# A later load of the second batch's expert results, and a copy that takes the attention numerators out of their bank

## The chip, the cores and the metric

The kernel runs on one core of one Trainium2 chip. The metric is the device time of one execution in microseconds. The engines are named as the profile names them: PE is TensorE, PEld its weight loads, DVE is VectorE, ACT is ScalarE, POOL is GpSimd and SP is SyncE, which issues most of the transfers.

## The reference, cut to what matters

`x` is (4, 512, 256) in float32. Two residual branches are added to it, one after the other. The first is a layer of experts followed by a linear attention, and the change lies where the one hands over to the other. The second (an attention with a field term, and two layers of local attention with a gated feed-forward) takes the larger part of the time and is not touched.

```python
def _L0_cond_ref(x, ...):                       # experts
    ...
    topk_w, topk_i = jax.lax.top_k(gate_w, TOP_K)               # 2 of 8 experts for each row
    cw = jnp.sum(jax.nn.one_hot(topk_i, E, dtype=x.dtype) * topk_w[..., None], axis=-2)
    h1 = jax.nn.relu(jnp.einsum('bsh,ehm->bsem', x, W1) + b1)
    h2 = jax.nn.relu(jnp.einsum('bsem,emn->bsen', h1, W2) + b2)
    out_e = jnp.einsum('bsen,enh->bseh', h2, W3) + b3
    return jnp.einsum('bseh,bse->bsh', out_e, cw)

def _L0_attn_ref(x, w_qkv, w_out, b_out, proj):  # linear attention, 8 heads of 32, blocks of 32 rows
    ...
    qp = jax.nn.elu(jnp.einsum('bhcsd,hdf->bhcsf', q, proj)) + 1.0
    kp = jax.nn.elu(jnp.einsum('bhcsd,hdf->bhcsf', k, proj)) + 1.0
    kv = jnp.einsum('bhcsf,bhcsd->bhcfd', kp, v)
    num = jnp.einsum('bhcsf,bhcfd->bhcsd', qp, kv)
    ksum = kp.sum(axis=3)
    z = 1.0 / (jnp.einsum('bhcsf,bhcf->bhcs', qp, ksum) + 1e-08)
    out = num * z[..., None]
    ...
    return out @ w_out.T + b_out

x = x + _L0_attn_ref(_L0_cond_ref(x, ...), ...)
x = x + _L0_ffn_ref(_L0_cond2_ref(x, ...), ...)
return x
```

## The kernel before

**The work and its stages.** There are four batches of 512 rows of 256 numbers, and each batch is four tiles of 128 rows (`NT`). From 0 to 317 us the experts run: rows are gathered for each expert, three layers are multiplied through, and GpSimd's indirect transfers (L1470) put each result row where it belongs in the DRAM tensor `ys`. While the last of these results travel, TensorE is kept busy by filler multiplications (`busy`, tile `pbusy`), which read `xres[0]`, batch 0's residual. From 317 to 349 us lies what this text calls the opening: the results are loaded back and batch 0's part of the linear attention begins. The linear attention fills 349 to 482 us, the attention with the field term 482 to 715, and the local attention with the feed-forward 715 to 1376.

**Loading and summing the results.** `results(b)` (L1525) makes the tiles `g0` and `g1` of 128 x 4 x 256, one for each of a row's two experts, and loads them from `ys` (L1532). Each tag has two buffers, so batches 0 and 1 can be loaded at once, while batch 2 waits until batch 0's tiles are free and batch 3 until batch 1's are. Batch 0 is loaded in four transfers of two tiles (256 KB each), those of `g1` on ScalarE's queue and those of `g0` on SyncE's; the others are loaded in two transfers of 512 KB, both on SyncE's. `weighted(b)` (L1536) then does, for each of the four tiles, one ScalarE multiplication (L1539, in place in `g0`, by the first expert's weight) and one VectorE operation that adds `g1` times the second weight and writes `y[b]`, the tile that the profile calls `ymoe` (L1540). At L1543 both batch 0's and batch 1's loads are issued, and after them batch 0's sums (L1544).

**The linear attention.** `front(b, d)` (L1556) is run for each batch: it makes the batch's sums (batch 0's are already made), issues the loads of batch b + 2, has GpSimd add the output bias to `xres[b]` (L1561, tile `xres`), transposes `y[b]` on TensorE (`pt` to `yT`) and multiplies by the weights (`pqk` to `qk`, `pv` to `v`). `evac` copies a PSUM bank to SBUF, in turn on ScalarE (L123) and on VectorE (L125). `features` multiplies each head's query or key by its projection (`pf`, two banks), and makes the feature of it with two ScalarE activations (`ex`, L1599 and L1600) and one VectorE operation that reads `pf` and `ex` (`f`, L1602). `scores` multiplies features by features (`psc`), and VectorE masks the product to the blocks (`sc`, L1612). `values(d, g)` takes a group of four heads: TensorE fills one bank with the numerators (`pn`) and one with the denominators (`pz`), ScalarE adds 1e-8 to the denominators (`z`, L1631), VectorE takes the reciprocal in place (L1636), and VectorE multiplies `pn` by it into `aT` (L1637). The last group of the last batch does these last two in halves. `tail` multiplies `aT` by the output weights (`pao`), and VectorE adds that to `xres` (L1647).

**What sets the order.** The order of TensorE's instructions is the program's own, pinned by `PE.in_order()` and `tc.keep_in_program_order`. The work of the next batch (`front`) and of the one before (`tail`) is handed out in steps by `beside(b)` between a batch's `features`, `scores` and `values`. Beside the last batch stand the first pieces of the next stage (`pck`, `pcq`, `pct`, `pcv`, and the field term's `fterm` operations on GpSimd, L390 and L391). The order on the other engines is chosen by a scheduler when the program is built, and it also chooses which bank a tile gets. All of `pt`, `pqk`, `pv`, `psc`, `pn`, `pz` and `pao` share four PSUM banks (kind `mm`); `pf` has its own two buffers of two banks. A matmul into a bank must wait for the last reader of what was in it.

## Time and profile before

| | |
|---|---|
| Time, median of three runs | 1381.41 us (1377.8 to 1935.3) |
| The profiled execution's own time | 1378.49 us |
| Its span in the trace | 1376.6 us |
| Mean granted TensorE clock | 0.994 of full speed |
| Instructions | 19525 |
| Bytes moved by the DMA engines | 94.74 MB |
| Busy in 317 to 349 us (32 us): PE, DVE, ACT | 28.95, 18.33, 20.03 us |
| Busy in 349 to 482 us (133 us): PE, DVE, ACT | 126.02, 96.95, 68.42 us |
| Busy in 482 to 715 us (233 us): PE, DVE, ACT | 230.03, 74.79, 137.61 us |

The profiled execution's time is the span of the trace and 1.9 us around it. The last three rows are read as what an engine worked within a stretch: the difference to the stretch's length is what it waited or stood without work. A name such as "pqk L78 <- DVE aT L1637" in a list of waits says that the instruction at line 78 which writes `pqk` was released by the VectorE instruction at line 1637 which writes `aT`. Line 78 is the helper that records every matmul, line 82 the one that records every transpose, so these are told apart by their tiles.

### The profile page before, as it was taken

The page shows a single profiled execution, that of the slowest core. Times are in us where ns is not written, and L with a number is a line of the kernel's source. Part 1 is how long each engine was busy: PE and PEld are TensorE (multiplying, and loading weights), DVE is VectorE, ACT ScalarE, POOL GpSimd, SP SyncE. Part 2 cuts the span into 40 slices and gives each one's busy share as a digit, 9 for nine tenths or more (in the row PEclk, how much of TensorE's full clock was granted, in tenths as well). Part 3 has the DMA queues.
Part 4 walks back from the last instruction along what each step waited for, and adds up shares of the span by engine and source line. Part 5 has one row for each costly group of instructions (what it writes and reads, how often), then busy time and mean ns, then how long its engine had stood idle before and what let it go on. Part 6 is the DMA issues. An engine that isn't in the chain of part 4 may idle for free.

```text
span 1376.6 us, 19525 instructions
## 1 busy us (share of the span) xinstructions
PE 1336.3 (97%) x7628; PEld 830.3 (60%) x7628; DVE 653.6 (47%) x1295; ACT 595.8 (43%) x1125; POOL 232.3 (17%) x223
## 2 busy tenths in 40 slices
PE   5999999999999999999999999999999999999998
PEld 4788888884566633433345556656555565556654
DVE  6222121225777743332237697653361777854421
ACT  4111111115555365565656755662222666574111
POOL 1324322211000021010103132000030322310110
PEclk8999999999999999999999999999999999999999
DMA  4577767543000000000220001211001010011000
GB/s 140 208 243 270 238 227 249 192 148 130 1 1 1 1 1 1 1 1 0 89 73 1 18 25 32 86 32 24 24 0 42 24 33 25 17 41 44 20 24 25
DMA packets 43086, 94.74 MB, mean 69 GB/s; under 512 B 9569, under 2 KB 25065, under 8 KB 40169
## 3 DMA queue, kind: packets, MB, share of 16 engines
q1 hardware_dynamic: 37560, 81.81, 18.3%
q0 software_dynamic: 3792, 10.24, 2.3%
q10 hardware_dynamic: 1632, 1.34, 0.3%
q8 instruction: 63, 1.03, 0.3%
q14 instruction: 39, 0.31, 0.1%
HBM read 84.08 MB, written 7.21 MB: 66 GB/s over the span
## 4 chain that ended last, share of the span: by engine, by line
PE 89%; DVE 5%; ACT 2%; DMA 1%; issue 1%; SPq 0%; POOLq 0%; POOL 0%; DVEq 0%
PE ph L78 14%; PE pdq L78 12%; PE pfy L78 6%; PE pug L78 5%; PE sc L78 5%; PE pua L78 5%; PE pv L78 5%; PE po L78 5%; PE pn L78 4%; PE pdy L78 4%; PE pds L78 4%; PE pz L78 2%; PE pqt L82 2%; PE pqk L78 1%; PE pck L78 1%
## 5 line engine op out<-in xcount | busy, mean ns | idle before, releaser
L78 PE MATMUL pdq<-wqkv,yT 128*128 128x512 f32 x384 | 177.1, 603 | 0.2 <-ACT yT L602 0.2
L420 ACT ACTIVATE cex<-sc 128x512 f32<-128x512 f32 x256 | 132.2, 603 | 85.5 <-PE sc L78 85.5
L78 PE MATMUL ph<-h,w 128*128 128x256 f32 (+1 forms) x704 | 132.8, 346 | 1.0 <-issue 1.0
L628 POOL TENSOR_TENSOR qr<-t,t 128x512 f32<-128x512 f32 x64 | 85.9, 1342 | 266.2 <-DVE t L625 225.2
L672 DVE TENSOR_TENSOR p<-p,lmask 128x384 f32<-128x384 f32 (+1 forms) x128 | 92.2, 735 | 69.4 <-ACT p L670 68.2
L78 PEld LDWEIGHTS ph<-h,w 128*128 128x128 f32 x704 | 116.1, 191 | 13.1 <-issue 1.3
L1402 ACT ACTIVATE h<-ph,w 128x256 f32<-128x256 f32 (+1 forms) x88 | 35.4, 438 | 190.7 <-PE ph L78 128.6
L78 PEld LDWEIGHTS pdq<-wqkv,yT 128*128 128x128 f32 x384 | 69.7, 190 | 78.4 <-issue 72.6
L670 ACT ACTIVATE p<-pds,ss 128x256 f32<-128x256 f32 (+1 forms) x256 | 96.1, 457 | 39.1 <-PE pds L78 30.7
L1404 DVE TENSOR_SCALAR h<-ph,w 128x256 f32<-128x256 f32 (+1 forms) x88 | 36.1, 438 | 160.3 <-PE ph L78 102.6
L78 PE MATMUL sc<-qm,kT 32*128 32x512 f32 x512 | 80.6, 639 | 0.0
L78 PE MATMUL pug<-hT,w 128*128 128x512 f32 x160 | 76.8, 602 | 0.0
L618 ACT ACTIVATE sq<-pdq 128x512 f32<-128x512 f32 x64 | 38.3, 598 | 85.4 <-PE pdq L78 47.7
L78 PE MATMUL pua<-hT,w 128*128 128x512 f32 x160 | 75.2, 592 | 0.0
L78 PE MATMUL ph<-xbT,w 128*128 128x256 f32 (+1 forms) x352 | 68.8, 347 | 0.6 <-ACT xbT L123 0.5
L78 PE MATMUL pv<-cex,v 128*32 128x512 f32 x512 | 68.6, 604 | 0.0
L390 POOL TENSOR_SCALAR fterm<-vw,faT 128x256 f32<-128x256 f32 x16 | 14.6, 925 | 316.2 <-DVE cr L380 316.2
L78 PE MATMUL po<-w,h 128*128 128x256 f32 x296 | 67.6, 379 | 0.0
L78 PE MATMUL pds<-qT,kT 64*128 64x256 f32 (+1 forms) x512 | 65.3, 375 | 0.0
L78 PEld LDWEIGHTS pds<-qT,kT 64*128 64x128 f32 x512 | 43.9, 186 | 32.9 <-issue 25.8
L78 PEld LDWEIGHTS ph<-xbT,w 128*128 128x128 f32 x352 | 58.5, 191 | 7.6 <-issue 0.8
L78 PE MATMUL pdy<-wo,oT 128*128 128x256 f32 x256 | 61.5, 386 | 0.0
(301 smaller groups left out, 2130.3 us busy)
## 6 DMA issues: line engine op xcount, KB each, us to landing
w<-in_moe_w_dram SPq DMA_DIRECT2D x22, 1024.0 KB
w<-in_moe_w_dram SPq DMA_DIRECT2D x22, 640.0 KB
w<-in_moe_w_dram SPq DMA_DIRECT2D x22, 516.0 KB
zb<-rows SPq DMA_DIRECT2D x32, 256.0 KB
g<-ys SPq DMA_DIRECT2D x6, 512.0 KB
wqkv<-in_f_wqkv_dram SPq DMA_DIRECT2D x2, 1536.0 KB
w<-in_f_w_dram SPq DMA_DIRECT2D x2, 1408.0 KB
out_dram<-yc SPq DMA_DIRECT2D x16, 128.0 KB
```

The lines of the kernel that those rows point to most:

```text
L78: cls._queue(nc.tensor.matmul(*args, **kw))
L82: cls._queue(nc.tensor.transpose(*args, **kw))
L390: nc.gpsimd.tensor_scalar_mul(fterm[:, t, :], vw, W["faT"][:, t, b : b + 1])
L420: nc.scalar.activation(ex[:, i, :], pss[2 * j + i], AF.Exp, scale=CHD**-0.5)
L618: nc.scalar.activation(sq, p3, AF.Square)
L628: nc.gpsimd.tensor_tensor(qr_t[:, s], t1, t2, ALU.add)
L670: nc.scalar.activation(p[:, at], pss[r][:, at], AF.Exp, scale=d.ss[:, 2 * u + jj, 1, 2 * c + r : 2 * c + r + 1])
L672: nc.vector.tensor_tensor(p[:, :n], p[:, :n], lmask[:, :n], ALU.mult)
L1402: nc.scalar.activation(dst, src, AF.Relu, bias=bias)
L1404: nc.vector.tensor_scalar(dst, src, bias, 0.0, ALU.add, ALU.max)
```

## The change

Two edits. First, batch 1's loads are issued behind batch 0's first two sums, where they were issued before any of the sums. Two one-element VectorE memsets into batch 1's tiles, pinned in program order, stand before the loads, so that the loads wait for them; and the load of `g1` goes to ScalarE's queue, where it was on SyncE's. `weighted` takes the tiles to be summed as an argument. Second, in `values`, ScalarE copies the numerators `pn` to `aT` in SBUF; VectorE multiplies `aT` in place by the reciprocals, where it multiplied from `pn`'s bank.

```diff
             def results(b):
                 gs = [gp.tile([128, NT, H], F32, tag=f"g{k}", name=f"g{k}", bufs=2) for k in range(2)]
+                if b == 1:
+
+                    for k in range(2):
+                        tc.keep_in_program_order(nc.vector.memset(gs[k][0:1, 0, 0:1], 0.0))
                 n = 2 if b == 0 else NT
...
-                        queue = nc.scalar if b == 0 and k == 1 else nc.sync
+                        queue = nc.scalar if b < 2 and k == 1 else nc.sync
...
-            def weighted(b, gs):
-                for t in range(NT):
+            def weighted(b, gs, at=range(NT)):
+                for t in at:
...
-            both = {b: results(b) for b in range(2)}
-            weighted(0, both[0])
+            both = {0: results(0)}
+            weighted(0, both[0], range(2))
+            both[1] = results(1)
+            weighted(0, both[0], range(2, NT))
...
                 nc.scalar.activation(z, pz, AF.Identity, bias=eps8)
 
+                nc.scalar.copy(d.aT[:, g, :], pn)
+
                 n = S // 2 if d is ds[-1] and g == 1 else S
                 for at in range(0, S, n):
                     half = slice(at, at + n)
                     nc.vector.reciprocal(z[:, half], z[:, half])
-                    nc.vector.tensor_tensor(d.aT[:, g, half], pn[:, half], z[:, half], ALU.mult)
+                    nc.vector.tensor_tensor(d.aT[:, g, half], d.aT[:, g, half], z[:, half], ALU.mult)
```

As the program is built, the order of TensorE's instructions is the same with the change as without it. On ScalarE the copy to `aT` stands ahead of `z` in all eight groups, although the code has it behind. On VectorE the memsets stand behind the last copy of the experts' stage (`faT`) and ahead of batch 0's third sum; batch 1's four sums stand ahead of the copy of `qk`; and in batch 3's first group both of the features `f` stand ahead of the addition to `xres`, where one of them stood behind it. With the change line numbers after L1525 move up: `aT` is copied at L1639 and multiplied at L1645, `z` is at L1637, its reciprocal at L1644, `f` at L1608, `sc` at L1618, `xres` at L1655, the loads at L1536 and the sums at L1544.

## The prediction

> **What bounds the kernel now.** The page first: TensorE is busy 97% of the span and carries 89% of the chain that ended last, so only a change in TensorE's own gaps or clock moves the end.

> ```profile
> PE 1336.3 (97%) x7628; PEld 830.3 (60%) x7628; DVE 653.6 (47%) x1295; ACT 595.8 (43%) x1125; POOL 232.3 (17%) x223
> PE 89%; DVE 5%; ACT 2%; DMA 1%; issue 1%; SPq 0%; POOLq 0%; POOL 0%; DVEq 0%
> ```

> Second, what TensorE waited for between 315 and 490 us, where both edits lie (columns: total us, times, longest). These six waits, 6.7 us in all, are what the change can aim at: under 0.5% of the span. Whatever it does, the reader should expect single microseconds.

> ```profile
> PE pt L82 <- DVE ymoe L1540: 2.3, 1, 2.3
> PE pqk L78 <- DVE aT L1637: 1.9, 2, 1.0
> PE pck L78 <- DVE aT L1637: 1.3, 1, 1.3
> PE pqk L78 <- DVE yT L125: 1.2, 2, 0.6
> ```

> Third, the opening, us by us (after the comma: busy of PE, PEld, DVE, ACT, POOL; clock; DMA share; GB/s), and the instructions in it.

> ```profile
> 321.00:322.00 1.00, 1.00 (x4) 0.28 (x2) 0.82 (x3) 0.59 (x3) 0.00 (x0) 1.00 1.08 374
> 323.00:324.00 1.00, 0.00 (x0) 0.00 (x0) 1.00 (x1) 0.01 (x1) 1.00 (x1) 1.00 1.09 385
> 325.00:326.00 1.00, 0.93 (x5) 0.88 (x5) 0.07 (x1) 0.61 (x2) 0.00 (x0) 0.50 0.00 0
> ```
> ```profile
> 322.06 2.34 POOL L1561 TENSOR_TENSOR xres<-xres,crows 128x1024 f32<-128x1024 f32 x1 [5.20 <-DMA g<-ys]
> 322.49 2.58 DVE L1540 SCALAR_TENSOR_TENSOR ymoe<-g,m,g 128x256 f32<-128x256 f32 x2 [0.35 <-ACT g L1539]
> 324.73 1.73 PE L82 MATMUL pt<-ident,ymoe 128*128 128x128 f32 x6 [2.29 <-DVE ymoe L1540]
> ```

> See that TensorE waits 2.29 us for batch 0's third and fourth sums, which take 2.58 together: one took 2.18 (the longest of the sixteen, whose median is 0.48) and ended 0.3 after GpSimd's addition, which it overlaps all along. The wait is for that addition, not for a load. After it the granted clock is 0.50 until 328.2, so eight pqk matmuls take 4.7 us where the next eight take 3.7.

> Fourth, the second numerator group of batch 0 (its twin is at 406-414), and the end of the stage.

> ```profile
> 371.05 0.69 ACT L1631 ACTIVATE z<-pz,eps 128x512 f32<-128x512 f32 x1 [3.06 <-PE pz L78]
> 371.77 3.35 DVE L1636 RECIPROCAL z<-z 128x512 f32<-128x512 f32 x1 [1.94 <-ACT z L1631]
> 375.22 0.69 DVE L1637 TENSOR_TENSOR aT<-pn,z 128x512 f32<-128x512 f32 x1
> 375.83 1.22 DVE L1602 SCALAR_TENSOR_TENSOR f<-pf,ex 128x1024 f32<-128x1024 f32 x1
> 376.96 0.68 DVE L125 COPY yT<-pt 128x512 f32<-128x512 f32 x1
> ...
> 375.97 1.12 PE L78 MATMUL pqk<-yT,awqkv 128*128 128x512 f32 x2 [0.96 <-DVE aT L1637]
> 377.70 1.12 PE L78 MATMUL pqk<-yT,awqkv 128*128 128x512 f32 x2 [0.60 <-DVE yT L125]
> ...
> 466.16 0.68 DVE L1647 TENSOR_TENSOR xres<-pao,xres 128x512 f32<-128x512 f32 x1
> 467.31 1.89 PE L78 MATMUL pcv<-cwqkv,xT 128*128 128x256 f32 x8
> ```

> See that the reciprocal, the multiplication, f and yT are one unbroken VectorE run from 371.77 on. TensorE waits for its second link (aT, which frees pn's bank) and then for its fourth (yT): taking the first wait away leaves the other. The last two rows show pcv starting 0.47 us after the xres that frees its bank.

> **The loads.** Removed: batch 1's transfers beside batch 0's. The microseconds from 318 moved 47, 303, 382 and 374 GB/s, 1.08 MB by 321.93, when batch 0's last half (1.05 MB in all) had landed: batch 1 had taken some 0.03 MB, 0.1 us. And the sum that follows waits for GpSimd, whose addition starts at 322.06 when TensorE's fillers end (321.96). Two memsets join VectorE after faT (321.98): a two-column operation takes 0.16, so 0.3 us, before a sum that is held to 324.4 anyway. If a memset is held too, that sum starts 0.3 later: 0 to +0.3; reductions and PSUM copies ran at their usual 0.69 beside GpSimd's work at 542-547, so I take 0.

> Added: later landings. SP's issue goes behind a memset, ScalarE's behind its fourth multiplication and a memset: about 322.4 and 322.9, where ScalarE is idle until 325.68, so its 0.47 is hidden. From batch 0's first issue (317.40) to its last landing (321.93) were 4.5 us; batch 1's is then at 327.0, where it was 324.6. Behind it on ScalarE: three multiplications (0.46 apart), then the qk copy, done by 329.4; TensorE's pf needs it at 330.95. Then a fourth, at 329.5, and batch 2's four (landing 329.2 as now, its SP issue still waiting for 325.1) until 331.6; ex, released by pf, starts at 332.13. Batch 3 is issued once batch 1's buffers are free: 330.5 for 328.8, so its last landing moves from 334.06 to at most 335.8; its first sum stands before f2 on VectorE, which ScalarE releases at 336.77. All hidden, with 1.5, 0.5 and 0.5 us of cover. If a cover goes, each us late is a us of TensorE. In return the VectorE qk copy moves from 331.44, behind batch 2's sums, to 331.05, but f2 is still ScalarE's: -0.4 to +1.5, taken -0.1. No indirect transfer on GpSimd's queue stands behind the loads.

> **The numerators.** Added: eight ScalarE copies of 128x512, 0.57 to 0.59 each by the qk and yT rows, ahead of z. The next ScalarE operation starts 0.48 after such a copy starts. pn ends 0.2 to 0.3 before pz, so z, and the VectorE run behind it, comes later by 0.26, 0.18, 0.19, 0.19 (pn ends at 370.76, 406.23, 441.79, 458.73; z started at 371.05, 406.60, 442.15, 459.09). The multiplication with both inputs in SBUF costs what it did: p<-p,lmask of 128x512 takes 0.69 too.

> By group, from each one's rows: the first groups of batches 0, 1 and 2 leave no TensorE gap and the shift ends in slack: 0. Second groups of batches 0 and 1: pqk's first half no longer waits 0.96, but its second half needs yT, now 0.26 (0.18) later: +0.26, +0.18. That of batch 2: pck's 1.27 goes, but pf's second half waits for the f that ended at 450.22: +0.19. First group of batch 3: the built order has xres behind the second f. It ended at 466.84 with 0.47 to spare before pcv; f's step is 1.13, plus 0.19: +0.85. Second group of batch 3: the second sc had waited for z (482.69); its bank now waits for the copy, 482.4: -0.3. So the waits named aT, 3.2 us, become waits for yT, f and xres.

> [...]

> Sum: -0.1 + 0.26 + 0.18 + 0.19 + 0.85 - 0.3 = +1.1. The profiled execution took 1378.5 (span 1376.6 and 1.9 around it), 2.9 under the median: 1379.6, given as 1380.

> **The rivals.**
> 1. *Clock.* The gaps at 375-378 and 410-413, now parted by a 0.96 us matmul, become one of 1.95. For: after 2.29 idle the clock was 0.50 for 3.2 us, 1.6 us lost. Against: gaps of 1.27 left it at 1.00. Both hit: +3.2, 1382.8. [...]
> 2. *Late loads.* Batch 2 or 3 lands past its cover and ScalarE holds qk or ex: +1 to +2.5, 1382. Against: 380 GB/s was free.
> 3. *Gain.* The aT waits go and nothing takes their place: -3.2, 1375.3. With the opening's too (2.3, and 1.6 of clock): 1371.4; against it, GpSimd's addition does not move.
> 4. *Other side: slower by over 2%.* The first merged gap (376) halves the clock and the gaps of the later groups, 17 to 18 us apart, keep it there. The stage holds 126 us of TensorE work from 349 to 482; each us of it run at half clock costs one more, so all of it +106 from 376 on (1485), and it decides from 28 us of such work. Against: the clock was 1.00 in every row from 330 to 480.
> That the edits do nothing: both are in the built order; 1378.5.

> **How the numbers follow.** Forecast 0.62, its own range 1377.5 to 1383; clock 0.12; late loads 0.13; gain 0.11; other side 0.02. Eight in ten: from the aT waits gone with half of the opening, 1374.5, to both clock hits with the late loads and the 2.9 of the median, 1386.5. Two per cent, about what a measurement can tell from no change, is 27.6 us: faster 0.01, same 0.97, slower 0.02.

> **What would show it.** Right: TensorE's waits name yT and f, no longer aT; pcv waits about 0.9 for xres; sum three still takes 2.2; z starts 0.2 after a copy. Wrong: a clock under 1.00 at 376-380; ScalarE idle before qk or ex for a load; an opening shorter by over 1 us.

## The result, and the profile after

| | before | with the change |
|---|---|---|
| Median of 12 runs | 1381.35 us | 1383.88 us |
| Ratio, with its 95% interval | | 1.0020 [1.0011, 1.0030] |
| The profiled execution, its span | 1378.49, 1376.6 us | 1383.97, 1382.2 us |
| Granted clock of that execution | 0.994 | 0.989 |

The change costs 0.2%: 2.5 us by the medians, 2.8 by the ratio, whose interval leaves out no change. One run of each kernel (1935.3 and 1422.7 us) was disturbed; it stands in the medians and not in the ratio. The page hardly differs; TensorE is still the chain:

```profile
PE 1340.6 (97%) x7628; PEld 831.7 (60%) x7628; DVE 653.9 (47%) x1297; ACT 599.1 (43%) x1133; POOL 232.0 (17%) x223
PE 89%; DVE 6%; ACT 2%; DMA 1%; issue 1%; SPq 0%; POOLq 0%; POOL 0%; ACTq 0%; DVEq 0%
```

TensorE's waits between 315 and 490 us, the view that answers to the one of before (total us, times, longest):

```profile
PE pqk L78 <- DVE yT L125: 4.0, 2, 2.0
PE pt L82 <- DVE ymoe L1544: 2.3, 1, 2.3
PE pf L78 <- DVE f L1608: 1.1, 3, 0.6
PE pcv L78 <- DVE xres L1655: 0.9, 1, 0.9
```

No wait names aT any more: the copy does empty the bank. But what stood behind it has moved up: 4.0 us for yT where aT and yT together had 3.1, f and xres in place of the 1.3 for aT, and the opening's 2.3 as it was. The place at 376, VectorE's run and then TensorE's rows:

```profile
372.54 3.35 DVE L1644 RECIPROCAL z<-z 128x512 f32<-128x512 f32 x1 [2.21 <-ACT z L1637]
375.93 0.69 DVE L1645 TENSOR_TENSOR aT<-aT,z 128x512 f32<-128x512 f32 x1
376.54 1.22 DVE L1608 SCALAR_TENSOR_TENSOR f<-pf,ex 128x1024 f32<-128x1024 f32 x1
377.67 0.68 DVE L125 COPY yT<-pt 128x512 f32<-128x512 f32 x1
```
```profile
375.35 1.02 PE L78 MATMUL pqk<-yT,awqkv 128*128 128x512 f32 x2
378.41 1.12 PE L78 MATMUL pqk<-yT,awqkv 128*128 128x512 f32 x2 [2.03 <-DVE yT L125]
```

The run of four links is as long as before (5.13 us from the first start to the last, before 5.19) and starts 0.3 later against TensorE. pqk's first half no longer waits, its second half waits for all of it: two waits of 0.96 and 0.60 have become one of 2.03.

That matters for the clock. Between 40 us and the last microsecond its record holds one stretch at half speed before the change (from 324.96) and five with it (from 43.62, 326.93, 415.67, 453.22 and 483.94), each 3.41 us long. Two of the five need not be the change's: 43.62 lies ahead of both edits, and `e6_open` below, which has neither edit, has one at 478.9, by the same small products as the one at 483.94. The one at 415.67, us by us (after the comma: busy of PE, PEld, DVE, ACT, POOL; clock; DMA share; GB/s):

```profile
415.00:416.00 1.00, 1.00 (x7) 0.47 (x8) 1.00 (x3) 0.58 (x1) 0.00 (x0) 0.84 0.00 0
416.00:417.00 1.00, 1.00 (x8) 0.00 (x0) 0.43 (x1) 0.07 (x1) 0.00 (x0) 0.50 0.00 0
...
419.00:420.00 1.00, 1.00 (x4) 0.50 (x3) 0.93 (x1) 0.97 (x3) 0.00 (x0) 0.96 0.00 0
```

And four stretches of 3.41 us that lie on the same grid (the half-clock stretches start at whole multiples of 3.41 us from each other); half clock followed the last three, and not the first:

```profile
374.71:378.13 3.42, 1.67 (x10) 0.84 (x8) 3.38 (x4) 2.55 (x3) 0.00 (x0) 1.00 0.01 2
412.26:415.67 3.41, 1.51 (x6) 0.75 (x10) 3.41 (x5) 1.16 (x2) 0.00 (x0) 1.00 0.01 2
449.81:453.22 3.41, 2.48 (x10) 0.77 (x10) 3.32 (x5) 2.43 (x3) 0.00 (x0) 1.00 0.00 0
480.53:483.94 3.41, 2.58 (x29) 1.86 (x21) 1.28 (x6) 0.78 (x2) 0.00 (x0) 1.00 0.02 5
```

TensorE was busy for 1.51 of the 3.41 us ahead of 415.67 (0.44) and the clock halved; the twin wait at 376 left 1.67 (0.49) in its stretch and the clock stayed. The two waits are alike (at its least, a stretch of 3.41 us laid over either is busy for 1.38 and 1.41); they differ in how they lie to the grid. The stretches ahead of 453.22 and 483.94 were 0.73 and 0.76 busy, so a low share of busy time is not all that half clock follows.

Where the 5.6 us between the two spans went is read from the same TensorE instruction in both traces (times are those of before's trace): with the change it starts later by 0.20 at 322 (the experts' stage), 0.50 at 339, 0.71 at 382, 2.57 at 417, 1.45 at 430 (slack took some back), 3.35 at 453, 4.18 at 471 and 5.49 at 486, and by no more after that. The larger jumps, at 417, 453 and 486, hold the half-clock stretches.

### The profile page after: what moved, and what is told of

Same layout as the page of the kernel before. It is cut to its first block, busy times and chain, and to the rows that moved or that the text cites. A ratio compares the mean times of both kernels' runs of the same rounds, so it can differ in the third digit from the quotient of the medians.

```text
span 1382.2 us, 19535 instructions
## 1 busy us (share of the span) xinstructions
PE 1340.6 (97%) x7628; PEld 831.7 (60%) x7628; DVE 653.9 (47%) x1297; ACT 599.1 (43%) x1133; POOL 232.0 (17%) x223
## 4 chain that ended last, share of the span: by engine, by line
PE 89%; DVE 6%; ACT 2%; DMA 1%; issue 1%; SPq 0%; POOLq 0%; POOL 0%; ACTq 0%; DVEq 0%
PE ph L78 14%; PE pdq L78 12%; PE pfy L78 6%; PE pug L78 5%; PE sc L78 5%; PE pua L78 5%; PE pv L78 5%; PE po L78 5%; PE pn L78 4%; PE pdy L78 4%; PE pds L78 4%; PE pz L78 2%; PE pqt L82 2%; PE pqk L78 2%; PE pf L78 1%; PE pur L78 1%
## 5 line engine op out<-in xcount | busy, mean ns | idle before, releaser
L78 PE MATMUL pdq<-wqkv,yT 128*128 128x512 f32 x384 | 177.1, 603 | 0.2 <-ACT yT L602 0.2
L78 PE MATMUL ph<-h,w 128*128 128x256 f32 (+1 forms) x704 | 132.8, 346 | 0.1
L78 PEld LDWEIGHTS ph<-h,w 128*128 128x128 f32 x704 | 116.2, 191 | 12.3 <-DVE h L1404 0.5
L78 PEld LDWEIGHTS pdq<-wqkv,yT 128*128 128x128 f32 x384 | 69.7, 190 | 78.4 <-issue 72.6
L78 PE MATMUL sc<-qm,kT 32*128 32x512 f32 x512 | 80.3, 639 | 0.0
L78 PE MATMUL pug<-hT,w 128*128 128x512 f32 x160 | 76.8, 602 | 0.0
L78 PE MATMUL pua<-hT,w 128*128 128x512 f32 x160 | 75.2, 592 | 0.0
L78 PE MATMUL ph<-xbT,w 128*128 128x256 f32 (+1 forms) x352 | 69.7, 351 | 0.5 <-ACT xbT L123 0.5
L78 PE MATMUL pv<-cex,v 128*32 128x512 f32 x512 | 68.6, 604 | 0.0
L78 PE MATMUL po<-w,h 128*128 128x256 f32 x296 | 67.6, 379 | 0.0
L78 PE MATMUL pds<-qT,kT 64*128 64x256 f32 (+1 forms) x512 | 65.3, 375 | 0.0
L78 PEld LDWEIGHTS pds<-qT,kT 64*128 64x128 f32 x512 | 43.9, 186 | 32.9 <-issue 25.0
L78 PEld LDWEIGHTS ph<-xbT,w 128*128 128x128 f32 x352 | 59.3, 194 | 7.2 <-ACT xbT L123 0.7
L78 PE MATMUL pdy<-wo,oT 128*128 128x256 f32 x256 | 61.5, 386 | 0.0
```

What stands on the lines that cost most here:

```text
L78: cls._queue(nc.tensor.matmul(*args, **kw))
```

## The experiments

Theory A: the change lengthens TensorE's waits by 1.1 us, as forecast, and adds half-clock stretches, about one in a mean execution. Theory B: the later loads are what costs. Each ratio is to runs of the kernel before on the same chip (29 to 35 of them), with 11 or 12 runs of the kernel itself.

**One edit at a time.** `e1_loads` takes out the second edit, `e2_copy` the first:

```diff
-                nc.scalar.copy(d.aT[:, g, :], pn)            # e1_loads, from the change
-  nc.vector.tensor_tensor(d.aT[:, g, half], d.aT[:, g, half], z[:, half], ALU.mult)
+  nc.vector.tensor_tensor(d.aT[:, g, half], pn[:, half], z[:, half], ALU.mult)
+                nc.scalar.copy(d.aT[:, g, :], pn)            # e2_copy, from before; aT as with the change
```

> Only the first edit: batch 1's loads behind batch 0's first two sums, on two queues; the numerators stay in their bank. Theory A (the change lengthens TensorE's waits in the linear attention by 1.1 us through the copy, and the merged waits starve TensorE for whole 3.41 us clock windows, which adds about one half-clock window of 1.7 us in a mean execution): this kernel stands where the kernel before does, ratio 0.999 to 1.001, one half-clock window in the opening and none from 349 to 490 us. Theory B (the later loads are what costs): it stands where the whole change does, +2 to +3 us, ratio 1.002.

> Only the second edit: ScalarE copies the numerators, VectorE multiplies in SBUF; the loads are as before. Theory A: the whole loss of the change, +1.5 to +4 us over before (ratio 1.001 to 1.003); TensorE waits twice about 2.0 us for yT; one to three half-clock windows from 349 to 490 us. Theory B: as before, ratio 1.000.

Measured: e1_loads 0.9999 [0.9986, 1.0012]; e2_copy 1.0015 [1.0004, 1.0026]. The loads cost nothing that shows (the interval leaves room for 1.7 us), the copy has the loss. Theory B falls. e2_copy's profile has the two waits of 2.0 for yT and half-clock stretches at 377.7 (its stretch was busy for 1.41 of 3.41) and 480.1.

**Fill the wait.** TensorE repeats a product whose result it overwrites, so that it is not idle:

```diff
                     ps = mmt("pqk")
+                    if b in (1, 2) and m == 0:               # e3_refill; (2, 3) in e3b_refill
+                        PE.matmul(ps, cw_["aqkv"][:, 0, 0:128], yT[:, 0, :], start=True, stop=True)
```

> The whole change, and TensorE repeats the first half product of pqk (two matmul instructions of 0.51 us) once ahead of its own in the fronts of batches 1 and 2, where it waits 2.0 us for yT: the idle time there falls to about 1.0 and the work that counts is not later. Theory A (a half-clock window follows a window of 3.41 us in which TensorE was busy for less than about half): no half-clock window at 376 to 381 and 412 to 420, the waits there 1.0 each, and 0.5 to 1.5 us less than the change in the mean. Rival (the clock falls by itself or for the length of one wait elsewhere): half-clock windows stay, time as the change or up to 1 us longer.

> The whole change, with the repeat of pqk's first half product now at both places where TensorE waits 2.0 us for yT (the fronts of batches 2 and 3; the first try had it at those of batches 1 and 2). It fills the wait and moves nothing that counts. Theory A (a half-clock window follows when TensorE was busy for less than about 0.48 of a 3.41 us stretch of a fixed grid): the least busy share of such a stretch around 376 and 412 rises from 0.41 to over 0.6, no half-clock window follows there, and the mean is 1 to 2 us below the change: ratio to before 1.0005 to 1.0012, what is left being the longer waits. Rival (those gaps have no part in the clock): half-clock windows there as with the change, ratio 1.002.

Measured: 1.0020 [1.0007, 1.0033] and 1.0020 [1.0008, 1.0032]. The first did not come down: one repeat stood at a place without a wait and cost 0.86, and the wait at 411, not filled, was followed by half clock at 414.98. In the second the two waits fell to 2.3 together and no half clock followed, in the profiled execution at least; but the mean time did not come down, so the two merged waits are not where most of the loss lies. That part of theory A's expectation failed. The mean clock of its runs, 0.9904, stayed under the 0.9918 of before on that chip, so clock was still lost in other executions or places. The run gave something else: an execution without one half-clock stretch from 349 to 490 us. The shift of TensorE's instructions against before goes from -1.26 at 350 to -0.15 at 486: the change's own waits are 1.11 us.

**Take out what TensorE waits for.** Both halves of yT on ScalarE, with the change and without:

```diff
-                    evac(yT[:, c, :], pt)
+                    if b:                                    # e4_yT from the change, e5_yT_nocopy from before
+                        turn[0] ^= 1
+                        nc.scalar.copy(yT[:, c, :], pt)
+                    else:
+                        evac(yT[:, c, :], pt)
```

> The whole change, and both halves of yT of batches 1 to 3 are copied by ScalarE (one of them was VectorE's, behind the reciprocal, the multiplication and f). Theory A (the wait that took the place of the one for aT is the one for yT, since VectorE's run was moved, not cut): the two waits of 2.0 us for yT go; pf then waits some 0.3 us for f; 0.7 us less at each of two places and fewer half-clock windows: 1.5 to 3 us below the change, about where before stands. Rival (TensorE then waits for f or sc just as long): time as the change.

> The kernel before, with both halves of yT of batches 1 to 3 copied by ScalarE; neither edit of the change. Beside the run with the change it tells what the copy of the numerators is worth once the wait behind it is gone. Theory A (VectorE's run of reciprocal, multiplication and f is what TensorE waits for in the end): the two waits of 0.96 for aT stay, the waits for yT go, pf waits up to 0.7 for f as there; within 1 us of that run, ratio 0.999 to 1.0005. Rival (the copy does take 0.9 us at each of the two places): 2 us over that run, ratio 1.001.

Measured: 0.9996 [0.9985, 1.0007] and 0.9996 [0.9987, 1.0005]. TensorE's waits in e4_yT from 345 to 490:

```profile
PE pf L78 <- DVE f L1612: 2.3, 4, 0.7
PE pcv L78 <- DVE xres L1659: 0.9, 1, 0.9
...
PE pqk L78 <- ACT yT L1576: 0.7, 2, 0.4
```

The 4.0 us for yT are gone and 2.3 for f are there: the next link of the same run. With this cover gone the copy is still worth nothing, as theory A had it. Note the second row: pcv waits 0.9 for xres as in the change, and yet the loss is gone.

**The opening.** The late fillers read the weights, so that GpSimd's addition to `xres[0]` runs in the experts' stage; alone (`e6_open`), on the change with yT on ScalarE (`e10_both`), and on the loads edit with yT on ScalarE but no copy (`e13_nocopy_both`):

```diff
-            busy(1)
+            busy(1, cw_["aqkv"][:, 0, :])                    # and the later busy(4), busy(2)
```

> The kernel before, with the last seven filler multiplications reading the weights awqkv instead of batch 0's residual, so that GpSimd's addition to that residual runs long before the opening; neither edit of the change. Theory A (the wait of 2.3 us at 322 is VectorE's third sum held up by that addition): the sum takes 0.5, the wait falls to about 0.7, the half-clock window after it goes in most executions: 2 to 3.5 us below before, ratio 0.998. Rival (the wait is for the loads, which the first edit of the change aims at): the wait stays over 2 us, ratio 1.000.

> The whole change with yT on ScalarE and with the fillers reading awqkv: the two repairs together. Theory A: the gains add: waits for yT under 0.5 each, the opening's wait about 0.7, half-clock windows only at the end of the linear attention if at all: 2.5 to 4.5 us below before, ratio 0.997 to 0.998. Rival (the second repair only moves the wait in the opening to a later load, since batch 1's loads are behind the first sums here): no better than with yT alone, ratio 0.9996.

> The first edit of the change alone (the loads), with yT on ScalarE and the fillers reading awqkv; the numerators stay in their bank. Theory A (once the wait behind it is gone, the copy of the numerators is worth nothing by itself, and the first edit is worth something only when GpSimd's addition is out of the opening): linear attention 1.1 us and opening 1.3 us shorter than before, ratio 0.9975 to 0.9988, as the kernel with the copy or up to 1 us faster. Rival (the copy is worth its waits for aT, 0.96 twice): 2 us over the kernel with the copy and z first.

Measured: 1.0005 [0.9994, 1.0016], 0.9994 [0.9981, 1.0007] and 0.9986 [0.9976, 0.9996]. The sums do get free: batch 0's third and fourth take 0.88 together in e10_both where they took 2.63 with the change, and TensorE's wait falls from 2.35 to 0.79. The change, and then e10_both:

```profile
322.64 2.63 DVE L1544 SCALAR_TENSOR_TENSOR ymoe<-g,m,g 128x256 f32<-128x256 f32 x2 [0.35 <-ACT g L1543]
```
```profile
321.24 0.88 DVE L1544 SCALAR_TENSOR_TENSOR ymoe<-g,m,g 128x256 f32<-128x256 f32 x2 [0.55 <-ACT g L1543]
...
325.71 1.31 ACT L1543 ACTIVATE g<-g,m 128x256 f32<-128x256 f32 x3 [2.54 <-DMA g<-ys]
...
327.54 1.13 PE L78 MATMUL pf<-qk,aproj 32*128 32x512 f32 x4 [0.61 <-ACT qk L123]
329.35 1.13 PE L78 MATMUL pf<-qk,aproj 32*128 32x512 f32 x4 [0.68 <-DVE qk L125]
```

The time of e6_open did not fall with it. There a wait of 2.26 for yT comes in its place, since ScalarE's copy to yT stands behind three multiplications that wait for batch 1's load (e6_open, ScalarE):

```profile
323.40 1.31 ACT L1539 ACTIVATE g<-g,m 128x256 f32<-128x256 f32 x3 [1.77 <-DMA g<-ys]
324.61 0.56 ACT L123 COPY yT<-pt 128x512 f32<-128x512 f32 x1
```

Where the loads edit is in (e10_both, e13_nocopy_both) ScalarE's order has yT first and that wait is 0.28. So the first edit removes a wait that only shows once GpSimd's addition is out of the way. It then brings one of its own, as the rival in e10_both's expectation had it: in e10_both ScalarE idles 2.54 for batch 1's later load, the copies of qk stand behind batch 1's multiplications and sums, and TensorE waits 0.61 and 0.68 for them, waits that e6_open does not have. e10_both gained less than expected, and these 1.3 us are part of it. e13_nocopy_both came as expected: with both repairs the kernel is no slower without the copy.

**Which order costs.** As built, the copy stands ahead of z, and batch 3's addition to xres behind both f. `e7_zfirst` pins z ahead of the copy (and the scheduler then put xres between the two f again); `e17_xres` puts xres back between the two f and leaves the copy ahead of z; `e18_z_only` puts z ahead of the copy and pins xres behind both f. The edit of e7_zfirst:

```diff
-                nc.scalar.activation(z, pz, AF.Identity, bias=eps8)
+                tc.keep_in_program_order(nc.scalar.activation(z, pz, AF.Identity, bias=eps8))
-                nc.scalar.copy(d.aT[:, g, :], pn)
+                tc.keep_in_program_order(nc.scalar.copy(d.aT[:, g, :], pn))
```

> The whole change with ScalarE's order pinned to z first, the copy to aT second, in every group. As built, this also puts one of batch 3's two f behind the addition to xres again. Theory A (the change's own waits are 1.1 us: z and all behind it 0.2 later at three places, and 0.85 where that addition stands behind both f; half-clock windows add the rest): the wait of pcv for xres goes, the waits for yT are 1.6 to 1.8 in place of 2.0, half-clock windows may still come at 376 and 412: ratio to before 0.9998 to 1.001. Rival (the loss lies in the merged waits and their clock alone): as the change, ratio 1.002.

> The whole change with one thing undone: in batch 3's first group the addition to xres stands between the two f again, as before the change (pinned); the copy stays ahead of z. Theory A (the loss is a sum of waits, 0.85 of it here): pcv's wait for xres goes, the waits of 2.0 for yT stay, 0.85 below the change: ratio to before 1.0008 to 1.0018. Rival (this place is the whole loss, the rest is slack): 1.0002 or less.

> The whole change with z ahead of the copy, but with the addition to xres kept behind both f of batch 3's first group (pinned): the other half of the run that put z first. Theory A: z starts 0.2 earlier at each second group, the waits for yT are about 1.8, pcv still waits 0.6 to 0.85 for xres: 0.6 to 1.2 below the change, ratio 1.0005 to 1.0015. Rival (the order of z and the copy is the whole loss): 0.9998.

| | xres behind both f | xres between them |
|---|---|---|
| copy, then z | the change 1.0020 [1.0011, 1.0030] | e17_xres 0.9998 [0.9987, 1.0009] |
| z, then copy | e18_z_only 1.0014 [1.0004, 1.0024] | e7_zfirst 0.9997 [0.9987, 1.0007] |

That place in the change, by time and all engines (the two f make one row of x2, xres follows, pcv waits for it), and then in e17_xres:

```profile
468.39 2.35 DVE L1608 SCALAR_TENSOR_TENSOR f<-pf,ex 128x1024 f32<-128x1024 f32 x2
...
470.66 0.68 DVE L1655 TENSOR_TENSOR xres<-pao,xres 128x512 f32<-128x512 f32 x1
...
471.39 0.92 PE L78 MATMUL pcv<-cwqkv,xT 128*128 128x256 f32 x3 [0.85 <-DVE xres L1655]
```
```profile
465.91 1.22 DVE L1611 SCALAR_TENSOR_TENSOR f<-pf,ex 128x1024 f32<-128x1024 f32 x1
...
467.04 0.68 DVE L1662 TENSOR_TENSOR xres<-pao,xres 128x512 f32<-128x512 f32 x1
467.64 1.22 DVE L1611 SCALAR_TENSOR_TENSOR f<-pf,ex 128x1024 f32<-128x1024 f32 x1
...
467.89 1.46 PE L78 MATMUL pcv<-cwqkv,xT 128*128 128x256 f32 x6
```

By the column, moving this one addition is enough to take the loss away: the two kernels with it between the f stand at before's time, although e17_xres still has both 2.0 us waits for yT. It is not the whole cause, for e4_yT and e10_both leave the addition behind both f, their pcv waits 0.9 and 0.8 for it, and they stand at before's time as well. Either repair does. Directly the place is worth 1.1: TensorE's shift against before goes from -0.86 at 440 to -0.15 at 488 in e3b_refill and from 0.67 to 0.26 in e17_xres, neither with half clock in between. The times of the two columns differ by 2.3 to 3 us, and e17_xres came out lower than theory A had it. Putting z first did not shorten the waits for yT either: they are 4.0 together in e7_zfirst and e18_z_only, where 1.6 to 1.8 each was expected. The mean clock goes with the column, though not by much: it is 0.0014 under that of before's runs on the same chip in e18_z_only, 0.0003 in e17_xres and 0.0006 in e7_zfirst. Why an addition 0.85 later should cost clock was not settled (the intervals of e17_xres and e18_z_only also touch).

**Put nothing behind the reciprocal.** `e12_zfirst_both` is e10_both with z first. `e16_late_recip` is e10_both with the reciprocal and the multiplication in quarters, two ahead of the next two f and two behind them; `e19_late_nocopy` is the same without the copy:

```diff
+                for at in range(0, S, S // 4):               # values() is a generator here
+                    yield
+                    half = slice(at, at + S // 4)
+                    tc.keep_in_program_order(nc.vector.reciprocal(z[:, half], z[:, half]))
...
+                        for _ in range(3):
+                            next(rec)                        # z, the copy, two quarters
                         next(fill, None)
                     if k + 1 < len(steps):
                         features(ds[b1], u1)                 # its f are pinned too
+                    run(rec)                                 # the other two
```

> The whole change with z ahead of the copy, yT on ScalarE and the fillers reading awqkv. Theory A: against the run with the two repairs alone the wait of pcv for xres (0.85) goes: linear attention 1.9 us shorter than before without a half-clock window in it, opening 1.3 shorter: ratio 0.997 to 0.9985. Rival (the copy behind z keeps a bank 0.6 us longer and psc waits for it instead): 0.999.

> The whole change with yT on ScalarE, the fillers reading awqkv, and the reciprocal and the multiplication cut into quarters of 128 columns, of which two stand ahead of the next two f and two behind them (pinned): since the numerators are out of their bank, nothing on TensorE waits for the reciprocal. Theory A (VectorE's unbroken run of 5 us is what TensorE waits for at 376 and 412, not the bank): the waits of pf for f fall from 0.6-0.7 to about 0.2, 0.7 us less at each of the two places than with yT on ScalarE alone, xres between the two f again (0.85): ratio 0.996 to 0.998. Rival (sc, now behind more small operations, holds up pn): no better than 0.999.

> The fastest kernel so far (loads, yT on ScalarE, fillers reading awqkv, reciprocal and multiplication in quarters around the next two f) without the copy: the multiplication reads pn in its bank. Theory A (the copy pays only where something is put ahead of the reciprocal, since the bank is then held longer): TensorE waits again for aT, 1 us or more at each of three places, 1.5 to 4 us over the kernel with the copy: ratio 0.998 to 0.9995. Rival (the quarters alone do it and the copy is idle): 0.9966 as with it.

Measured: e12_zfirst_both 0.9998 [0.9987, 1.0009], 2 to 4 us short of what was expected (pcv's wait went, but TensorE's waits for f rose from 2.3 in e10_both to 3.3, and half clock followed the longest, 1.1, at 413.37; what lengthened them stays open); e16_late_recip 0.9966 [0.9955, 0.9978], 4.7 us under before and the fastest kernel of the study; e19_late_nocopy 1.0009 [0.9999, 1.0018], so that the copy is worth 0.0043 of 1379, 5.9 us, in this order. In the two traces, neither with half clock from 349 to 490, TensorE's instructions drift apart by 5.6 us over that stretch, so the waits there hold it. VectorE in e16_late_recip, where both f now stand ahead of the second pair of quarters:

```profile
371.74 0.95 DVE L1649 RECIPROCAL z<-z 128x128 f32<-128x128 f32 x1
...
373.33 1.23 DVE L1612 SCALAR_TENSOR_TENSOR f<-pf,ex 128x1024 f32<-128x1024 f32 x1 [0.31 <-ACT ex L1610]
...
375.67 1.22 DVE L1612 SCALAR_TENSOR_TENSOR f<-pf,ex 128x1024 f32<-128x1024 f32 x1
376.81 0.94 DVE L1649 RECIPROCAL z<-z 128x128 f32<-128x128 f32 x1
```

The four largest of TensorE's waits from 345 to 470, in e16_late_recip and then in e19_late_nocopy:

```profile
PE pn L78 <- ACT yT L1576: 0.8, 1, 0.8
PE pqk L78 <- ACT yT L1576: 0.7, 2, 0.4
PE pn L78 <- DVE sc L1622: 0.6, 3, 0.2
PE psc L78 <- DVE sc L1622: 0.4, 1, 0.4
```
```profile
PE pqk L78 <- ACT yT L1576: 2.4, 2, 1.2
PE pn L78 <- DVE sc L1622: 1.7, 8, 0.3
PE pck L78 <- ACT xT L293: 1.2, 1, 1.2
PE pao L78 <- DVE xres L1658: 1.0, 3, 0.3
```

With the copy no wait for aT is left, nor one for f among these. Without it the waits are longer, and cost more than theory A's 1.5 to 4 us; but they are not put down to aT, where it had expected them: at 373 pqk's first half, which needs only the first half of yT (copied at 369.27), starts at 373.86, when the copy of the second half has ended. That fits a bank taken over from pt while pn's was still held, and was not tried by itself.

## Why the prediction was wrong

The mechanism in the linear attention was right, nearly term by term; the time it was turned into was not, and the clock had no term.

- *The numerators* held. The waits for aT went and became waits for yT, f and xres, as said. Second groups of batches 0 and 1: +0.26 and +0.18 forecast, 0.21 and 0.20 found (0.50 to 0.71 in the change, -1.06 to -0.86 in e3b_refill); batch 2: +0.19, found 0.28; last group: -0.3, found -0.3. At pcv the wait is the forecast 0.85, but there TensorE falls back by 1.11 in e3b_refill, and the first numerators of batch 3 (456 to 459 us of before's trace) had come 0.36 sooner, which was not forecast. These terms were to give +1.18 and give 1.11; that they agree so well is in part luck.
- *The loads* held: 0.9999. The third sum stayed blocked (the pair took 2.63), and batch 1's first multiplication began at 327.17, behind a landing forecast for 327.0. The two memsets took 0.06 together, not 0.3. Over the opening TensorE's shift was +0.30 with the change and -0.50 in e1_loads, where half clock fell on other instructions; the -0.1 of the sum is too small to be told from that. Of the eight multiplications from SBUF, seven lie where GpSimd stood idle (160.36 us ahead of 484.95) and took 0.68 each in the mean; the last one's halves (492.07) began when the fterm work had ended (491.3) and took 0.69 together.
- *The step that failed* is the last of the sum: "The profiled execution took 1378.5 [...], 2.9 under the median: 1379.6, given as 1380." A loss of 1.1 was so given as a time under the median of before. That execution was one of the quick ones, with the highest clock of all: of 132 runs of before measured later, 25 had 0.994 and took 1376.8 in the mean, 15 had 0.989 and took 1381.7, and all of them 1378.9. A difference of two executions had to be put on the median: 1382.5, inside the stated range. The measured 1383.9 is 1.4 above that. The sum had nothing for the clock, and there the rest was most likely lost; no run shows it by itself.
- *The clock* was a rival at 0.12, priced at two places only. It is a term that each execution pays by chance (the mean clock of the 132 runs of before lies between 0.989 and 0.994), and the copy raised it: over the runs of e2_copy the mean clock was 0.9896, over the 35 of before on that chip 0.9915, an estimated 2.6 us (0.0019 of 1379), of which slack gives some back. Slid over the change's trace, a stretch of 3.41 us is busy for as little as 0.41 around 376 and 412, and at each of the two some 0.55 of all positions of the grid would give a stretch under 0.48; in the trace of before the least is 0.54. And two more places lost clock, 450 and 480, which the prediction did not name; why the one at 450 did is open. The row (2.29 us idle, then half clock) was read as the length of one wait; over the 3.41 us ahead of that half clock TensorE was busy for 0.32.
- *Late loads*, *gain* and *the other side* did not come: no load ended a wait of ScalarE's on the path, aT's waits were taken over, and half clock never lasted beyond one stretch there.
- *The range of eight in ten* does not come out of the terms that it names: 1375.3 less half of the opening's 3.9 is 1373.4, where 1374.5 was given, and 1382.8 with 1 to 2.5 for late loads and 2.9 is 1386.7 to 1388.2, where 1386.5 was. The result lies within either.

## What to carry to other kernels

Emptying a bank early paid here only where something then moved ahead of the slow instruction that held it: while the reciprocal kept its place the copy cost 2 us by itself and was worth nothing with yT on ScalarE; it was worth 5.9 once f could pass the reciprocal. When a built order changes, look at each instruction that it moves: putting one addition back between two others took this loss away, by a way that is open in part. Set a difference that was worked out on one profiled execution against the median, and look at that execution's clock first.
